# A gated recurrence with residual: x turned on VectorE from small pieces, biases spread by TensorE

## The chip, the core and the metric

The kernel runs on one core of one Trainium2 chip. A core has a matrix engine (TensorE, PE in the profile; its weight loads are PEld), a vector engine (VectorE, DVE), an activation engine (ScalarE, ACT), a general engine (GpSimd, POOL) and SyncE (SP), which here only issues transfers. Each engine runs its own list of instructions in order and waits on semaphores for the others. ACT, POOL and SP each have a queue of transfers, all served by the same 16 DMA engines. Matrix results land in PSUM, everything else lives in SBUF, both with 128 partitions. The metric is the device time of one execution in microseconds. Before the change it is 1333.65 us (median of 3 runs, 1333.27 to 1333.81).

## What is computed

```python
def step(h, inp):                      # x_t, h: 64 x 512; 128 steps
    x_t, prop = inp
    comb = jnp.concatenate([x_t, h], axis=-1)
    z = jax.nn.sigmoid(comb @ Wz + bz)
    r = jax.nn.sigmoid(comb @ Wr + br)
    comb2 = jnp.concatenate([x_t, r * h], axis=-1)
    h_cand = jnp.tanh(comb2 @ Wh + bh)
    h_new = (1.0 - z) * h + z * h_cand
    h_next = jnp.where(prop, jnp.tanh(h_new @ Wp + bp), h_new)
    return (h_next, h_new)             # prop: every fourth step but the last
out = x + transpose(ys)                # x: 64 x 128 x 512, all f32
```

Each weight matrix is 1024 x 512: the upper half meets x, the lower half meets h. Wp is 512 x 512.

## The kernel before

**Layout.** The batch is 64, so a step's 64 x 512 values are kept as 128 partitions x 256 columns: partition s*64+b holds half s of row b. `S = 2` halves, `C = 2` blocks of 128 columns in each, `Q4 = 4` steps to a group. A product needs its left operand turned (columns on the partitions), so every x, h and r*h has to be transposed. `turn` (L212) does it on PE: 8 transposes of bf16 words into the PSUM banks `turn_ps`, and a copy by DVE or ACT. The other half of each `turn_ps` bank, `act_ps`, holds the results of sigmoid and tanh.

**x-part.** The products of x with the upper weights don't depend on the recurrence. They are cut into units and put in `queue`; `fill(n)` issues n of them wherever PE would else wait for the recurrence, `read_out()` issues the copies that empty the four `scratch` banks. Steps 0 to 3 use plain products (`plain`, L428, with readouts L436 and L441 that add the biases). Groups 1 and later use sums and differences of blocks, with fewer products (`batch`, L509; readouts L541 to L552), whose input sums run on POOL (`four`, `sum_raw12`, `sum_raw34`, `sum_s12`) and whose output sums too (`pair_left`, `outer_*`). The weight sums `tw` and `tt` are made during the first steps by DVE (`sum_outer`, L320 to L322; `sum_outer_1`, L326) and POOL (`sum_inner`, L329 to L331).

**Recurrence.** In step t: the R product (four k blocks, `product` at L203), then sigmoid on ACT (L741) and r*h on DVE (L742); three of the four Z products; the turn of r*h and DVE's copies into `rhT` (L210); the last Z product; z, 1-z (L767, L768) and `keep` (L769); units; the H product; tanh (L802) and h on DVE (L803, L808); units; the turn of h, one half copied by DVE, the other by ACT. `seed` (L411) has ACT copy the x-part of the next step into the PSUM slot on which the recurrent products add. The order of all engines is written by hand; each waits only where data or a buffer demands it.

**x, three ways.** The x of steps 0 to 7 (groups 0 and 1, tiles `xr`) is turned on PE by `turn_x` (L243), steps 0 and 1 before the first product, step 2 in step 0 between Z products (L754), steps 3 to 5 in step 0, 6 and 7 in step 1. From group 2 on x takes a path in three pieces: `words_x` (L255) splits each f32 into two 16-bit planes (ACT for groups 2 and 3, POOL later), `planes_x` (L268) turns the planes by one DMA transpose from SP, and `join_x` (L278, L283) has ACT weave the two planes into `xT`. Groups 2 and 3 are loaded early into tiles borrowed from `mb` (`early`), the later ones into one tile `xs`. The inner function `join(n)` (L709) is called at two places of a step, `join(0)` behind r*h and the R seed, `join(1)` behind `keep`, and turns one x at steps with certain numbers `u` in a cycle of eight.

**Loads of the start.** In order on SP: x of steps 0 and 1 (half on ACT's queue), the upper weights of R, Z, H in two pieces of 512 KB each (one on ACT's queue), the lower weights of R and Z, x of steps 2 and 3, the lower weights of H, x of steps 4 to 7, group 2, Wp, the bias of Wp, group 3, group 4. POOL's queue carries, behind a copy into `held` that waits for the first x, h0 (two halves of 64 KB) and the three gate biases, each broadcast from one row to 64 partitions, twice 64 KB each. `idle` (L179) issues matmuls of zeros until the first data arrive. On SP a transfer is issued when the eighth before it on the two hardware queues has landed, which is seen in the issue times (L96 at 14.82 us, when the load of the upper Wh had landed).

Of the kernel before, what the change touches and what calls it, by code (L numbers as in the profile page):

```python
# [9 lines left out]
F32 = mybir.dt.float32  # L10
BF16 = mybir.dt.bfloat16
U16 = mybir.dt.uint16
# [5 lines left out]
def kernel(  # L18
# [41 lines left out]
    R, Z, H_ = range(3)  # L60
# [15 lines left out]
    ones = const.tile([1, B], F32, name="ones")  # L76
# [5 lines left out]
    wx = const.tile([P, K, 3, H], F32, name="wx")  # L82
    wh = [const.tile([P, K, H], F32, name=f"wh_{i}") for i in range(3)]
    wp = const.tile([P, K, H], F32, name="wp")

    tw = {n: const.tile([P, S, S, 3, P], F32, name=f"tw_{n}") for n in (2, 3, 4)}
    tt = const.tile([P, 7, 3, S, 3, P // 2], F32, name="tt")
    gates_in = (Wr, Wz, Wh)
    def load_x(tile_, t0, n, j=0):
        for s in range(S):  # L90
            nc.sync.dma_start(
                out=tile_[s * B : (s + 1) * B, j : j + n, :], in_=x[:, t0 : t0 + n, ts(s, N)]
            )
# [12 lines left out]
    h_init = two.tile([P, N], F32, tag="h", name="h_init")  # L106
    bias_in = const.tile([P, 4, N], F32, name="bias")
# [11 lines left out]
    def load_bias(i, eng):  # L119
        for s in range(S):  # L120
            eng.dma_start(
                out=bias_in[s * B : (s + 1) * B, i, :],
                in_=(br, bz, bh, bp)[i][ts(s, N)]
                .rearrange("(o n) -> o n", o=1)
                .broadcast_to([B, N]),
            )


    held = const.tile([1, 1], F32, name="held")
    nc.gpsimd.tensor_copy(held, xr[0][0:1, 0, 0:1])  # L130
    for s in range(S):
        nc.gpsimd.dma_start(out=h_init[s * B : (s + 1) * B, :], in_=h0[:, ts(s, N)])
    for i in (R, Z, H_):
        load_bias(i, nc.gpsimd)
    for i in range(3):
        for k in (0, 2):
            load_w(wh[i], gates_in[i][D:, :], k, k + 2, nc.sync)
        if i == Z:
            load_x(xr[0], 2, 2, 2)

    dummy = const.tile([1, 1], F32, name="dummy")
    nc.scalar.activation(dummy, ones[:, 0:1], AF.Sigmoid)
    new_xr(1)
    load_x(xr[1], 4, 4)
    early = {}
    for g in (2, 3):
        early[g] = mbp.tile([P, 2, 2, 3, P], F32, tag="mb", name=f"early_{g}").rearrange(
            "p a b c d -> p (a b c d)"
        )[:, : Q4 * N].rearrange("p (t n) -> p t n", t=Q4)
    load_x(early[2], 8, 4)  # L150
    load_w(wp, Wp, 0, 4, nc.sync)
    load_bias(3, nc.sync)
    load_x(early[3], 12, 4)


    rc = ps_c.tile([P, 2, N], F32, name="rc")
# [14 lines left out]

    def cut(ps):
        return ps.rearrange("p (c n) -> p c n", c=C)

    bias0 = bias[:, 0, 0:3, :]
    bias_d = const.tile([P, 3, P], F32, name="bias_d")
# [32 lines left out]
    def copy(eng, dst, src):  # L209
        (eng.copy if eng is nc.scalar else eng.tensor_copy)(dst, src)  # L210
# [21 lines left out]


    xT = {}
    xs = {}
    xw = {}
    xv = {}

    def new_xT(g):
        if g not in xT:  # L240
# [2 lines left out]
    def turn_x(t, eng=nc.scalar):  # L243
        g, i = divmod(t, Q4)
        new_xT(g)
        src = xr[g] if g < 2 else early[g]
        for c in range(C):
            turn(src[:, i, :], xT[g][:, i], c, f"xT_{t}", eng)

    def load_xs(g):  # L250
        if g * Q4 < T:
            xs[g] = one.tile([P, Q4, N], F32, tag="xs", name=f"xs_{g}")
            load_x(xs[g], g * Q4, Q4)

    def words_x(g, i):  # L255

        if g * Q4 >= T:
            return
        if g not in xw:
            xw[g] = one.tile([P, Q4, 2, N], U16, tag="xw", name=f"xw_{g}")  # L260
        src = (early if g < 4 else xs)[g]
        copy(
            nc.scalar if g < 4 else nc.gpsimd,
            xw[g][:, i],
            src[:, i, :].bitcast(U16).rearrange("p (n w) -> p w n", w=2),
        )

    def planes_x(g):  # L268

        if g * Q4 >= T:  # L270
            return
        xv[g] = one.tile([P, Q4, 2, C, P], U16, tag="xv", name=f"xv_{g}")
        nc.sync.dma_start_transpose(
            out=xv[g].rearrange("p t w c n -> p (t w c) n"),
            in_=xw[g].rearrange("p t w n -> p (t w n)"),
        )

    def join_x(g, i):  # L278

        if g * Q4 >= T:  # L280
            return
        new_xT(g)
        nc.scalar.copy(  # L283
            xT[g][:, i].bitcast(U16).rearrange("p c (n w) -> p w c n", w=2), xv[g][:, i]
        )


# [362 lines left out]
    idle(4)  # L650
    turn_x(1, nc.vector)
    idle(8)
    nc.gpsimd.tensor_sub(bias_d, bias[:, 1, 0:3, :], bias0)
    h = h_init
    hT = new_T("hT", "hT_init")
    both = [plain(0), plain(1)]
    for e in range(3):
        for us in both:
            queue.extend(us[4 * e : 4 * e + 4])
        fill(4)  # L660
        if e == H_:
            read_out()
            seed(R, 0)
            seed(Z, 0)
            seed(H_, 0)
        fill(4)
        if e == Z:
            for c in range(C):
                turn(h, hT, c, "hT_init", nc.vector)
# [4 lines left out]
    for t in range(T):  # L674
# [48 lines left out]
        for k in ORDER:  # L723
            product(slots[R], hT, wh[R], k)
        if t < 2:
            if t:
                turn_x(6)
        if t == 1:
            for i in (5, 7):
                sum_inner(i, nc.gpsimd)  # L730
# [20 lines left out]

        for k in ORDER[: 2 if thin else 3]:
            product(slots[Z], hT, wh[Z], k)
        if t == 0:  # L754
            turn_x(2)
        rhT = new_T("rhT", f"rhT_{t}")
        for c in range(C):
            turn(rh, rhT, c, f"rhT_{t}", nc.vector)
# [9 lines left out]
        nc.scalar.activation(slots[Z], slots[Z], AF.Sigmoid, scale=-1.0)  # L768
        nc.vector.tensor_mul(keep, slots[Z], h)  # L769
        join(1)  # L770
        seed(Z, t + 1)
        if prop:
            nc.scalar.copy(cut(slot_p), bias[:, :, 3, :])
# [2 lines left out]
        if t == 0:  # L776
            sum_outer()
            for i in (6,):
                sum_inner(i, nc.gpsimd)
                sum_inner_1(i, nc.gpsimd)  # L780
        if t == 1:
            for n in range(4):
                words_x(2, n)
            planes_x(2)
        elif t == 2:
            for n in range(1, 4):
                join_x(2, n)
            for n in range(2):
                words_x(3, n)
        if not thin:  # L790
            fill(places[0])
        if t == 0:
# [18 lines left out]
        if t == 2:  # L811
            for n in range(2, 4):
                words_x(3, n)
            planes_x(3)
        read_out()
        fill(places[0] if thin else 5 if places[1] > 6 else 4)
        if t == 1:
            turn_x(7)
            sum_raw34(1)
        h = h_new  # L820
        if not last:
            hT = new_T("hT", f"hT_{t}")
            turn(h, hT, 0, f"hT_{t}", nc.vector)
            fill(places[1] if thin else 1 if places[1] > 6 else 2)
            turn(h, hT, 1, f"hT_{t}", nc.scalar)
        if t == 0:
            fill(3)
            turn_x(4)
            fill(3)
        else:  # L830
            fill(places[2] if thin else places[1] - 6)
        if t == 0:
            sum_outer_1()
            for i in (1, 2, 3):
# [11 lines left out]
                turn(h, hT, c, f"hpT_{t}", (nc.vector, nc.scalar)[c])  # L846
            fill(behind[1] if thin else 2)
        if t == 0:
            turn_x(5)
            sum_raw12(1)  # L850
        elif t == 3:
            pair_left(1, 8, 9)
            pair_right(1, 8, 11)
# [38 lines left out]
            sum_s12(even + 2)  # L892
        if t == 2:
            pair_right(0, 1, 10)
        if pair >= 0:
            if u in (1, 2):
                for n in range(2):
                    words_x(even + 2, 2 * (u - 1) + n)
            if u in (5, 6):
                for n in range(2):  # L900
                    words_x(odd + 2, 2 * (u - 5) + n)

        if not last:
            nc.gpsimd.tensor_add(xr[g][:, j, :], xr[g][:, j, :], h_new)  # L904
# [4 lines left out]
        n = 0  # L909
# [14 lines left out]
        if t == 0:  # L924
# [47 lines left out]
```

## Time and profile before

| what | value |
|---|---|
| median of 3 runs | 1333.65 us (1333.27 to 1333.81) |
| profiled execution | 1334.15 us, span 1332.3 us |
| granted clock of TensorE | 0.999 |
| matrix instructions | 15320 |
| DMA: share of 16 engines, all queues | q1 24.7%, q8 0.6%, q10 0.2%, q0 0.1% |
| `join_x` (L283) on ACT | 120 copies, 765 ns each, 91.4 us |
| `words_x` (L210) on POOL | 112 copies, 613 ns each, 65.3 us |
| `words_x` (L210) on ACT | 8 copies, 612 ns each, 4.4 us |
| `turn_x` (L219, from xr) on PE | 64 transposes |
| DMA transpose xv<-xw | 30, 4.3 us from issue to landing (median) |
| biases, POOL's queue | 6 transfers of 64 KB, 6.6 to 6.7 us from issue to landing |

The span is the time from the first to the last instruction of the program; the time of an execution is some 2 us longer. Rows of the profile name a line of the kernel, an engine, an operation and its tiles (written tile first), the number of instructions, their busy time and the mean time of one, and the engine's idle time before them with what ended it. q1 is SP's queue, q10 ACT's, q0 POOL's. The start of a matmul is measured; its end is modelled, since matmuls overlap, so the distance between starts (0.108 us for 256 columns in a run of sixteen that takes 1.73 us) says more of the cost than the duration.

### The profile page before, as it was taken

The page shows a single profiled execution, that of the slowest core. Times are in us where ns is not written, and L with a number is a line of the kernel's source. Part 1 is how long each engine was busy: PE and PEld are TensorE (multiplying, and loading weights), DVE is VectorE, ACT ScalarE, POOL GpSimd, SP SyncE. Part 2 cuts the span into 40 slices and gives each one's busy share as a digit, 9 for nine tenths or more (in the row PEclk, how much of TensorE's full clock was granted, in tenths as well). Part 3 has the DMA queues.
Part 4 walks back from the last instruction along what each step waited for, and adds up shares of the span by engine and source line. Part 5 has one row for each costly group of instructions (what it writes and reads, how often), then busy time and mean ns, then how long its engine had stood idle before and what let it go on. Part 6 is the DMA issues. An engine that isn't in the chain of part 4 may idle for free.

```text
span 1332.3 us, 37617 instructions
## 1 busy us (share of the span) xinstructions
PE 1321.7 (99%) x15320; PEld 1110.8 (83%) x15320; DVE 702.6 (53%) x1870; ACT 635.4 (48%) x1860; POOL 934.9 (70%) x1139
## 2 busy tenths in 40 slices
PE   8999999999999999999999999999999999999998
PEld 5788888888888888888788888888888888888765
DVE  3555555555555555555555555555555555555444
ACT  1554454454544544545444454545545444554433
POOL 4877876777777668776787767786777687767400
PEclk9999999999999999999999999999999999999999
DMA  9322232131221222213122221223212222131300
GB/s 283 55 49 49 49 65 64 33 65 41 57 65 33 66 52 46 65 44 82 37 43 55 64 65 33 59 40 65 65 33 65 49 50 65 33 76 37 98 23 17
DMA packets 119277, 77.79 MB, mean 58 GB/s; under 512 B 65984, under 2 KB 114240, under 8 KB 119104
## 3 DMA queue, kind: packets, MB, share of 16 engines
q1 hardware_dynamic: 118352, 74.14, 24.7%
q8 instruction: 121, 1.98, 0.6%
q10 hardware_dynamic: 496, 0.72, 0.2%
q0 software_dynamic: 256, 0.52, 0.1%
q14 instruction: 52, 0.43, 0.1%
HBM read 42.86 MB, written 16.78 MB: 45 GB/s over the span
## 4 chain that ended last, share of the span: by engine, by line
PE 96%; DMA 2%; DVE 1%; ACT 1%; issue 0%; SPq 0%; DVEq 0%; ACTq 0%
PE rc L194 33%; PE zp L194 20%; PE scratch_q L194 11%; PE scratch_r L194 10%; PE scratch_x L194 10%; PE scratch_a L194 6%; PE turn L219 5%; DMA xr<-in_x_dram 1%; DMA wx<-in_L_cond_Wz_dram 1%; ACT xw L210 0%; ACT xT L283 0%; DVE h L808 0%; DVE turn L803 0%; SPq L96 0%; DVE mb L550 0%
## 5 line engine op out<-in xcount | busy, mean ns | idle before, releaser
L194 PE MATMUL rc<-wh,rhT 128*64 128x256 f32 x2048 | 246.0, 379 | 0.0
L582 POOL TENSOR_TENSOR cp<-mb,mb 128x768 f32<-128x768 f32 x74 | 134.4, 1817 | 102.4 <-ACT rc L411 54.7
L194 PE MATMUL zp<-wh,hT 128*64 128x256 f32 x1536 | 204.3, 379 | 0.0
L194 PEld LDWEIGHTS rc<-wh,rhT 128*64 128x64 f32 x2048 | 168.3, 137 | 40.5
L194 PE MATMUL rc<-wh,hT 128*64 128x256 f32 x1536 | 186.3, 383 | 0.2
L904 POOL TENSOR_TENSOR xr<-xr,h 128x256 f32<-128x256 f32 x127 | 92.5, 728 | 105.3 <-DVE h L808 105.3
L194 PEld LDWEIGHTS rc<-wh,hT 128*64 128x64 f32 x1536 | 121.1, 137 | 36.5 <-issue 9.7
L582 POOL TENSOR_TENSOR cp<-mb 128x768 f32<-128x768 f32 x46 | 83.5, 1815 | 95.1 <-ACT rc L411 93.7
L210 DVE COPY rhT<-turn 128x256 uint16<-128x256 uint16 x256 | 97.6, 420 | 82.2 <-PE turn L219 81.1
L194 PEld LDWEIGHTS zp<-wh,hT 128*64 128x64 f32 x1536 | 118.8, 137 | 25.2
L803 DVE TENSOR_TENSOR turn<-turn,z 128x128 f32<-128x128 f32 x256 | 75.5, 295 | 120.7 <-ACT turn L802 119.0
L741 ACT ACTIVATE turn<-rc 128x128 f32<-128x128 f32 x256 | 55.2, 260 | 171.2 <-issue 111.5
L210 ACT COPY hT<-turn 128x256 uint16<-128x256 uint16 x127 | 47.3, 372 | 165.7 <-DVE hT L210 127.8
L582 POOL TENSOR_TENSOR mb<-mb,mb 128x768 f32<-128x768 f32 x58 | 105.3, 1816 | 9.6 <-DVE mb L552 9.6
L411 ACT COPY rc<-cp 128x256 f32<-128x256 f32 x256 | 96.4, 377 | 26.7 <-DVE cp L436 13.6
L550 DVE TENSOR_TENSOR mb<-scratch_r,cq 128x384 f32<-128x384 f32 (+1 forms) x105 | 58.3, 555 | 92.7 <-ACT cq L549 92.7
L802 ACT ACTIVATE turn<-rc 128x128 f32<-128x128 f32 x256 | 55.5, 260 | 105.3 <-PE rc L194 104.0
L543 DVE TENSOR_TENSOR cx<-scratch_r,cx 128x384 f32<-128x384 f32 (+1 forms) x105 | 58.3, 556 | 88.8 <-ACT cx L541 88.8
L767 ACT ACTIVATE z<-zp 128x256 f32<-128x256 f32 x128 | 49.1, 383 | 94.3 <-PE zp L194 94.2
L283 ACT COPY xT<-xv 128x512 uint16<-128x512 uint16 x120 | 91.4, 765 | 0.0
L808 DVE TENSOR_TENSOR h<-turn,keep 128x128 f32<-128x128 f32 x254 | 74.1, 292 | 15.6 <-DVE turn L803 0.5
L219 PEld LDWEIGHTS <-h 128*64 128x64 bf16 x1016 | 67.6, 110 | 14.0 <-DVE h L808 7.4
(161 smaller groups left out, 3018.0 us busy)
## 6 DMA issues: line engine op xcount, KB each, us to landing
xr<-in_x_dram SPq DMA_DIRECT2D x62, 256.0 KB, 4.1
out_dram<-xr SPq DMA_DIRECT2D x62, 256.0 KB, 3.4
xs<-in_x_dram SPq DMA_DIRECT2D x56, 256.0 KB, 4.2
wx<-in_L_cond_Wz_dram SPq DMA_DIRECT2D x2, 512.0 KB, 8.1
wx<-in_L_cond_Wh_dram SPq DMA_DIRECT2D x2, 512.0 KB, 11.4
wh<-in_L_cond_Wr_dram SPq DMA_DIRECT2D x2, 512.0 KB, 13.2
wh<-in_L_cond_Wz_dram SPq DMA_DIRECT2D x2, 512.0 KB, 15.2
wh<-in_L_cond_Wh_dram SPq DMA_DIRECT2D x2, 512.0 KB, 12.3
```

The lines of the kernel that those rows point to most:

```text
L194: nc.tensor.matmul(ps[s * B : (s + 1) * B], lhsT=lhs, rhs=rhs(s), start=start, stop=True, skip_group_check=True,)
L210: (eng.copy if eng is nc.scalar else eng.tensor_copy)(dst, src)
L219: nc.tensor.transpose(pt[s * B : (s + 1) * B, w, :], words.rearrange("p (n w) -> p w n", w=2)[:, w, :], ident16,)
L283: nc.scalar.copy(xT[g][:, i].bitcast(U16).rearrange("p c (n w) -> p w c n", w=2), xv[g][:, i])
L411: nc.scalar.copy(cut(slots[i]), G[t][:, :, i, :])
L543: nc.vector.tensor_add(T2[n][:, :nm], r_ps[:, :nm], T2[n][:, :nm])
L550: nc.vector.tensor_add(blocks()[:, :nm, 0, 1], r_ps[:, :nm], q2[:, :nm])
L582: nc.gpsimd.tensor_add(dst, a, b)
L802: nc.scalar.activation(pc, slots[H_][:, ts(c, P)], AF.Tanh)
L803: nc.vector.tensor_mul(pc, pc, z[:, ts(c, P)])
L808: nc.vector.tensor_add(h_new[:, ts(c, P)], pc, keep[:, ts(c, P)])
L904: nc.gpsimd.tensor_add(xr[g][:, j, :], xr[g][:, j, :], h_new)
```

## The change

Seven edits:

1. The x of groups 1 and later is loaded by `load_xs` in small pieces: eight transfers for a group, each from 32 rows of the batch into 32 partitions, in runs of 32 f32 (128 bytes), into two alternating tiles of the tags `xs0` and `xs1`. The runs are laid so that each square of 32 x 32 needs only to be turned in itself.
2. `join_x` turns one step's x by one `transpose` on DVE (128 x 256 f32 in squares of 32 x 32) from `xs` into `xT`. `words_x`, `planes_x`, the tiles `early`, `xw` and `xv` and the DMA transposes go.
3. `turn_x` stays for steps 0 to 3 alone. That of step 2 moves from behind three Z products to behind the R product of step 0. Steps 4 and 5 become `join_x` at the end of step 0, 6 and 7 become `join_x` behind `keep` in step 1, with `sum_raw34(1)`.
4. The three gate biases are loaded by POOL as single rows into one partition of `tt`, first on its queue. `spread`, called behind the first eight units, multiplies a column of ones with them into the banks `scratch[3]` and `scratch[1]`, and ACT copies the three results into `bias`. `bias_d` moves behind it.
5. `held`, and with it the load of h0, waits for the first upper weights of R instead of the first x.
6. The x of steps 2 and 3 is loaded ahead of the lower weights of Z instead of behind them.
7. Groups 1 and 2 are loaded into `xs` behind the lower weights of H; then Wp, its bias, and the plain x of steps 4 to 7 for the residual. Groups 3 and 4 are loaded at the ends of steps 1 and 2, the later ones at `u` 3 and 6 as before.

```diff
+    bias_row = tt.rearrange("p a b c d e -> p (a b c d e)")[0:1, : 3 * H].rearrange(
+        "p (i n) -> p i n", i=3
+    )
...
+    for i, b in enumerate((br, bh, bz)):
+        nc.gpsimd.dma_start(out=bias_row[:, i, :], in_=b.rearrange("(o n) -> o n", o=1))
 
     held = const.tile([1, 1], F32, name="held")
-    nc.gpsimd.tensor_copy(held, xr[0][0:1, 0, 0:1])
+    nc.gpsimd.tensor_copy(held, wx[0:1, 1, R, 0:1])
     for s in range(S):
         nc.gpsimd.dma_start(out=h_init[s * B : (s + 1) * B, :], in_=h0[:, ts(s, N)])
-    for i in (R, Z, H_):
-        load_bias(i, nc.gpsimd)
     for i in range(3):
         for k in (0, 2):
             load_w(wh[i], gates_in[i][D:, :], k, k + 2, nc.sync)
-        if i == Z:
+        if i == 0:
             load_x(xr[0], 2, 2, 2)
...
+    def load_xs(g):
+        if g * Q4 < T:
+            xs[g] = one.tile([P, Q4, S * C, 2, 32], F32, tag=f"xs{g % 2}", name=f"xs_{g}")
+            for r in range(4):
+                for bh in range(2):
+                    nc.sync.dma_start(
+                        out=xs[g][ts(r, 32), :, :, bh, :].rearrange("p t k e -> p (t k) e"),
+                        in_=x[ts(bh, 32), g * Q4 : (g + 1) * Q4, :].rearrange(
+                            "b t (k r e) -> r b (t k) e", k=S * C, r=4
+                        )[r],
+                    )
+
+    load_xs(1)
+    load_xs(2)
+    load_w(wp, Wp, 0, 4, nc.sync)
+    load_bias(3, nc.sync)
     new_xr(1)
     load_x(xr[1], 4, 4)
-    early = {}
...
-    load_x(early[2], 8, 4)
-    load_w(wp, Wp, 0, 4, nc.sync)
-    load_bias(3, nc.sync)
-    load_x(early[3], 12, 4)
...
+    def spread(bank, rows, which):
+
+        bank = bank.rearrange("p (i n) -> p i n", i=2)
+        n = len(which)
+        for s in range(S):
+            nc.tensor.matmul(
+                bank[s * B : (s + 1) * B, 0:n, :],
+                lhsT=ones,
+                rhs=bias_row[:, rows, ts(s, N)],
+                start=True,
+                stop=True,
+            )
+        for j, i in enumerate(which):
+            nc.scalar.copy(bias_in[:, i, :], bank[:, j, :])
...
     def join_x(g, i):
 
         if g * Q4 >= T:
             return
         new_xT(g)
-        nc.scalar.copy(
-            xT[g][:, i].bitcast(U16).rearrange("p c (n w) -> p w c n", w=2), xv[g][:, i]
+        nc.vector.transpose(
+            out=xT[g][:, i].rearrange("p c (s b) -> p s c b", s=S),
+            in_=xs[g][:, i].rearrange("p (s c) h e -> p s c (h e)", s=S),
         )
...
+        if e == R:
+
+            spread(scratch[3], slice(0, 2), (R, H_))
+            spread(scratch[1], slice(2, 3), (Z,))
+            nc.gpsimd.tensor_sub(bias_d, bias[:, 1, 0:3, :], bias0)
...
         for k in ORDER:
             product(slots[R], hT, wh[R], k)
         if t < 2:
-            if t:
-                turn_x(6)
+            if t == 0:
+                turn_x(2)
...
         nc.vector.tensor_mul(keep, slots[Z], h)
         join(1)
+        if t == 1:
+            join_x(1, 2)
+            join_x(1, 3)
+            sum_raw34(1)
...
-        if t == 1:
-            for n in range(4):
-                words_x(2, n)
-            planes_x(2)
-        elif t == 2:
+        if t == 2:
             for n in range(1, 4):
                 join_x(2, n)
-            for n in range(2):
-                words_x(3, n)
...
-        if t == 1:
-            turn_x(7)
-            sum_raw34(1)
...
-        if t == 0:
-            fill(3)
-            turn_x(4)
-            fill(3)
-        else:
-            fill(places[2] if thin else places[1] - 6)
+        fill(places[2] if thin else places[1] - 6)
...
         if t == 0:
-            turn_x(5)
+            join_x(1, 0)
+            join_x(1, 1)
             sum_raw12(1)
...
-        if t == 0:
-            load_xs(4)
+        if t in (1, 2):
+            load_xs(t + 2)
         if pair >= 0:
             if u == 3:
-                planes_x(even + 2)
                 load_xs(odd + 2)
             elif u == 6:
-                planes_x(odd + 2)
                 load_xs(even + 4)
```

The steps of the schedule that call `join` (its table of steps and `u`) are unchanged.

More of the change, by code (lines that the diff above doesn't have):

```diff
@@ L142 @@
     nc.scalar.activation(dummy, ones[:, 0:1], AF.Sigmoid)
+    xs = {}
+    def load_xs(g):
[13 more added lines that the diff above has]
+    load_bias(3, nc.sync)
     new_xr(1)
     load_x(xr[1], 4, 4)
-    early = {}
[L146 to L149, printed above, removed]
-    load_x(early[2], 8, 4)
-    load_w(wp, Wp, 0, 4, nc.sync)
-    load_bias(3, nc.sync)
-    load_x(early[3], 12, 4)
     rc = ps_c.tile([P, 2, N], F32, name="rc")
@@ L234 @@
     xT = {}
-    xs = {}
-    xw = {}
-    xv = {}
     def new_xT(g):
@@ L245, in turn_x @@
         new_xT(g)
-        src = xr[g] if g < 2 else early[g]
+        src = xr[g]
         for c in range(C):
             turn(src[:, i, :], xT[g][:, i], c, f"xT_{t}", eng)
[L250 to L276, printed above, removed]
     def join_x(g, i):
@@ L652 @@
     idle(8)
-    nc.gpsimd.tensor_sub(bias_d, bias[:, 1, 0:3, :], bias0)
     h = h_init
@@ L753 @@
             product(slots[Z], hT, wh[Z], k)
-        if t == 0:
-            turn_x(2)
         rhT = new_T("rhT", f"rhT_{t}")
@@ L810 @@
             seed(H_, t + 1)
[L811 to L814, printed above, removed]
         read_out()
         fill(places[0] if thin else 5 if places[1] > 6 else 4)
-        if t == 1:
-            turn_x(7)
-            sum_raw34(1)
         h = h_new
@@ L894 @@
             pair_right(0, 1, 10)
[L895 to L901, printed above, removed]
         if not last:
@@ L923 @@
             load_x(xr[g + 1], (g + 1) * Q4, Q4)
-        if t == 0:
-            load_xs(4)
+        if t in (1, 2):
+            load_xs(t + 2)
         if pair >= 0:
             if u == 3:
-                planes_x(even + 2)
                 load_xs(odd + 2)
             elif u == 6:
-                planes_x(odd + 2)
                 load_xs(even + 4)
```

## Prediction

> **What bounds the kernel now.** I read the busy shares first, then a table of stretches, then the chain of waits at the start, then the timeline of single engines.
>
> ```profile
> PE 1321.7 (99%) x15320; PEld 1110.8 (83%) x15320; DVE 702.6 (53%) x1870; ACT 635.4 (48%) x1860; POOL 934.9 (70%) x1139
> ...
> 8.00:12.50 4.50, 3.98 (x38) 2.37 (x37) 0.00 (x0) 0.00 (x0) 0.56 (x2) 1.00 1.07 298
> 12.50:25.00 12.50, 10.65 (x98) 6.06 (x99) 3.29 (x8) 1.87 (x6) 9.20 (x10) 1.00 1.06 338
> 25.00:44.00 19.00, 18.65 (x218) 14.72 (x220) 15.22 (x27) 6.35 (x21) 9.61 (x12) 1.00 0.81 176
> ...
> 100.00:420.00 320.00, 320.00 (x3756) 276.29 (x3753) 172.77 (x461) 157.15 (x460) 237.48 (x290) 1.00 0.25 54
> ```
>
> The stretch rows give length, then busy time and count of PE, PEld, DVE, ACT and POOL, granted clock, DMA share, GB/s. From 100 us on PE fills the stretch, and the waits view has no wait of PE between 100 and 1240 us. Whatever the change takes from ACT or POOL there is worth nothing; only PE instructions that go, or new waits of PE, count. Before 25 us the DMA share is full and PE has holes: the start is bound by loads.
>
> ```profile
> 2.94 9.46 DMA wx<-in_L_cond_Wz_dram
> ...
> 12.42 12.43 DMA xr<-in_x_dram
> ...
> 25.32 0.38 ACT xT L210
> ...
> 45.27 2.18 ACT xw L210 x4
> ```
>
> The chain (start, length, what) runs through Wz, the x of steps 2 and 3, the ACT copy that turns x of step 2, and ACT's `words_x`.
>
> **The loads of the start.** The biases are now 384 KB of broadcast on POOL's queue; the change reads three rows of 2 KB. What that frees is seen in three stretches:
>
> ```profile
> 9.00:14.00 5.00, 4.48 (x42) 2.74 (x40) 0.00 (x0) 0.00 (x0) 0.00 (x0) 1.00 1.06 272
> 15.00:20.00 5.00, 4.88 (x52) 2.85 (x48) 2.80 (x6) 1.06 (x3) 4.30 (x5) 1.00 1.05 386
> 25.00:29.00 4.00, 3.65 (x44) 2.83 (x46) 2.23 (x5) 1.68 (x5) 0.68 (x1) 1.00 1.13 221
> ...
> q1 hardware_dynamic: 473, 0.91, 70.7%
> q0 software_dynamic: 229, 0.45, 35.0%
> ```
>
> The two queue rows are those of 9 to 14 us: SP's queue moved 0.91 MB there while POOL's moved 0.45. In 15 to 20 us SP's alone moved 1.92 MB. So 0.45 MB of POOL's traffic cost SP's stream 1.01 MB, at 386 GB/s 2.6 us; all 0.52 MB cost about 3.0, and the biases' three quarters 2.2 us. By bytes alone 0.39 MB would be 1.0 us; I take 2.2, the measured loss, and keep 1.0 as the low end.
>
> Now the last load that step 0 waits for. Before: Wz's second recurrent half lands at 23.69, x of steps 2 and 3 at 24.85 (landings read from the trace). The change swaps them; the sum ahead of the last of them is the same, so the last now lands at 24.85 - 2.2 = 22.65. PE before:
>
> ```profile
> 23.73 1.08 PE L194 MATMUL zp<-wh,hT_init 128*64 128x256 f32 x8 [1.13 <-DMA wh<-in_L_cond_Wz_dram]
> ...
> 24.98 0.42 PE L219 MATMUL turn<-ident,xr 128*64 128x128 bf16 x8 [0.17 <-DMA xr<-in_x_dram]
> ...
> 25.75 0.58 PE L219 MATMUL turn<-ident,rh 128*64 128x128 bf16 x8 [0.35 <-ACT xT L210]
> ...
> 26.57 0.38 PE L194 MATMUL scratch_q<-wx,xT 128*64 128x256 f32 x1
> ```
>
> After: PE starts at 7.82 as before (Wr; POOL's bulk traffic began only at 8.3). The eight units of the R gate take 2 x 1.73 (16 matmuls take 1.73 in the chain), to 11.28. `spread` adds two pairs of matmuls, one of 512 columns, one of 256: a pair of 256 takes 1.73/4 = 0.43, so 0.86 + 0.43 = 1.3, to 12.6. Z units 3.46, hT_init 0.22, H units 3.46, R product of step 0 1.73, to 21.45; `turn_x(2)`, whose x is there by then, 0.22; first Z product 0.43, to 22.1. There it waits for Wz until 22.7 (landing plus 0.05). Two Z products 0.86, turn of rh 0.25, last Z product 0.43: filling starts at 24.24 instead of 26.57. **Gain 2.3.** The 1.3 us of `spread` lie ahead of the wait and are hidden, 0.55 to spare. Without any wait PE could not be there before 23.75 (rh's own path through ACT, now behind `turn_x(2)`'s two copies): ceiling 2.8. With 1.0 for the biases: 1.1.
>
> Moved past POOL's queue: `h_init` waits for Wr (7.8) instead of x (4.2). It landed 5.8 after issue, so 13.7 and 14.4; PE wants it at 16.04. Cost 0, 1.6 us to spare. `bias_d` and the three ACT copies (0.38 each) end by 14; their first reader is at 17.
>
> **PE instructions that go.** `turn_x` of steps 4 to 7 goes: 8 transposes each, 0.22 us in the chain. **Gain 4 x 0.22 = 0.88**, certain. The ACT copies behind the one of step 7 also held PE: the last matmul ahead of it starts at 49.07, turn of h at 50.23, 1.16 us for 0.16 + 0.30 of work. The wait is shared with h, which came late because ACT ran `words_x` up to 47.45, and with it the readouts `cx`, `cq`, tanh, and then DVE. With those copies gone, `cx` is read when its units end, h is ready before PE asks. **Gain 0.70** (low end 0). The same at step 2: PE waits for h at 67.66 and 68.19, excess 0.41, behind `words_x` at 63.98 to 65.1. **Gain 0.41** (low end 0). The wait at 75.65 for DVE's L550 stays: it hangs on the rhT copies.
>
> **What DVE gets.** 124 turns of 128x256 f32. The trace has no such operation; nearest are DVE operations of 128x256 at 0.42 (L769, L441). Bounds: 0.33 (only the 256 columns and a little) and 0.84 (two passes). I take 0.42: 52 us in all, DVE from 53% to 57%. Where do they stand? `join(0)` is between rh and the copies of rhT, `join(1)` behind keep:
>
> ```profile
> 453.54 0.49 DVE L742 TENSOR_TENSOR rh<-turn,hprop 128x128 f32<-128x128 f32 x2 [0.40 <-ACT turn L741]
> 454.65 0.76 DVE L210 COPY rhT<-turn 128x256 uint16<-128x256 uint16 x2 [0.62 <-PE turn L219]
> 455.89 0.42 DVE L769 TENSOR_TENSOR keep<-zp,hprop 128x256 f32<-128x256 f32 x1 [0.48 <-ACT zp L768]
> ```
>
> The hole ahead of rhT is 0.62, and the H product that reads rhT starts at 455.29, 0.22 behind the first copy's end (455.07). So a turn of up to 0.84 costs nothing there; behind keep DVE is idle 1.29 until 457.60. Steady state: 0.
>
> At the end of step 0 it is tighter. `join_x(1, 0)` and `(1, 1)` stand behind the weight sums:
>
> ```profile
> 39.56 1.02 DVE L334 TENSOR_TENSOR wx<-wx 128x384 f32<-128x384 f32 x2
> ...
> 41.10 0.41 DVE L441 TENSOR_TENSOR cp<-scratch_x,bias 128x256 f32<-128x256 f32 x1
> 42.48 0.49 DVE L742 TENSOR_TENSOR rh<-turn,h 128x128 f32<-128x128 f32 x2 [0.97 <-ACT turn L741]
> ```
>
> DVE is busy without a break from 36.55 to 41.51, so all shifts by 2.3. Sums end at 38.27, joins at 39.1, readouts L436 and L441 at 40.1, rh at 40.35 and 40.6. PE, 2.3 + 0.44 earlier, ends the R product at 38.74 and three Z products at 40.04, and turns rh's second half only at 40.65. **Loss 0.45** (0 with short turns, 1.3 with turns of 0.84). POOL's s12r, s34r and `pair_left` follow 1.2 to 3.5 us earlier, ahead of their readers.
>
> **The small pieces.** One group of four steps is 4,096 packets of 128 B on 16 engines, 256 each. Nearest row: the DMA transpose of 48 to 52 us, 256 B each:
>
> ```profile
> q1 hardware_dynamic: 2080, 0.52, 94.3%
> ```
>
> 94.3% of 16 x 4 us over 2,080 packets is 29 ns each; 256 x 29 = 7.4 us a group. The load of Wh ends at 29.14 - 2.2, about 26.6 to 27; with 1.5 us to land, group 1 is there at 35.5, wanted at 38.3 by DVE; group 2 at 43, wanted at 50.6 (first join of step 2). Hidden, and 7.4 us in 41 later. The Trainium skill speaks against it: "DMA: Bandwidth & Descriptors", Specifications, wants at least 512 B for line rate and has smaller ones do a read-modify-write. Taken as twice the row, an estimate, 58 ns: group 1 at 43, group 2 at 58, and DVE, with PE behind it, waits 7 us in all. By the row 0, by the rule a loss of 7. I take the row, which has small packets with all that they cost; no run yet shows 128 B from HBM. The low end is bytes alone, 1.4 us a group; the high end 82 ns, what a packet cost at 25 to 29 us, where x was read in 1 KB rows (1.13 x 64 us over 886 packets).
>
> **Sum.** 2.3 + 0.88 + 0.70 + 0.41 - 0.45 = 3.84. The profiled execution took 1334.15 (span 1332.3), half a us over the median of 1333.65; so 1330.3 by the one, **1329.8** by the median. Own range: best 2.8 + 0.88 + 1.11 = 4.8, worst 1.1 + 0.88 - 1.3 = 0.7; likely 1328.9 to 1331.2.
>
> **Rivals.**
> - *Small pieces late (slower).* The DVE queue stands behind group 1, then group 2, at step 2. It decides from (50.6 + 3.8 - 28.1)/0.512 = 51 ns a packet; at 58 ns 7 late less 3.8 is about 1337, at 82 near 1349. For: x in long strides is slow already (221 against 386 GB/s). Against: 256 B packets at 29 ns. 15%.
> - *DVE turns over 0.84.* At 1.2 us each of 60 `join(0)` holds rhT 0.36: 22 us, 1352. Against: nothing of 256 columns on DVE takes over 0.42. 5%.
> - *The start does not follow* (h_init late, or Wz gains by bytes alone), and the two h waits stay: 0.7 to 2.6 us, about 1331.8. 20%.
>
> The forecast has 60%. A difference of 0.2% is 2.7 us, about what can be told from none. Faster 0.60; same 0.19, the third rival; slower 0.21, the first two and a little of the unforeseen. The range 1328.6 to 1336 holds forecast, third rival and the mild part of the first.
>
> **What would show it.** Right: filling of step 0 starts near 24.2; no `xw`, `xv` rows; no wait of PE at 49 and 67; a wait of about 0.4 for rh near 40; DVE turns near 0.42; x group 1 landed by 38, group 2 by 50. Wrong: DVE idle behind a DMA of xs, packets of 128 B over 51 ns, or PE waits that recur past 100 us.

## The result and the profile after

| | before | after |
|---|---|---|
| median of 14 runs each | 1333.72 us (1332.73 to 1336.55) | 1330.46 us (1329.96 to 1331.19) |
| ratio | | 0.9974, 95% interval 0.9967 to 0.998 |
| profiled execution | 1334.15 us, span 1332.3 | 1330.92 us, span 1328.9 |

The changed kernel is 3.26 us faster by the medians and 3.4 by the spans of the two profiled executions; 3.84 was forecast. Its profiled execution has the longest span of its 14 (1327.6 to 1328.9, median 1328.2). The busy shares, from the page of the changed kernel:

```profile
PE 1320.0 (99%) x15296; PEld 1114.5 (84%) x15296; DVE 748.0 (56%) x1994; ACT 552.5 (42%) x1727; POOL 871.0 (66%) x1024
```

ACT lost 83 us of work, POOL 64, DVE gained 45, and PE, which sets the time, lost 1.7. The table of stretches of the changed kernel, columns as before:

```profile
8.00:12.50 4.50, 3.27 (x30) 2.02 (x32) 0.00 (x0) 0.00 (x0) 0.00 (x0) 1.00 1.06 356
12.50:25.00 12.50, 12.50 (x128) 7.87 (x130) 3.66 (x10) 3.34 (x11) 9.90 (x10) 1.00 1.07 300
25.00:44.00 19.00, 18.90 (x200) 12.96 (x198) 16.51 (x32) 4.71 (x15) 9.54 (x11) 1.00 0.61 133
...
100.00:420.00 320.00, 320.00 (x3754) 276.31 (x3752) 184.22 (x492) 137.53 (x429) 219.72 (x261) 1.00 0.19 40
```

The steady stretch is as full as before. From 12.5 to 25 us PE, which had been idle for 1.85 us, is now never idle; the loads no longer hold it. The hole has moved to 8 to 12.5 us, where PE lost 0.52 before and loses 1.23 now. The waits of PE between 0 and 100 us in the changed kernel (total, times, longest; left out is one of 1.2 for DVE's zeros, which all these kernels have):

```profile
PE scratch_q L224 <- DMA wx<-in_L_cond_Wr_dram: 1.7, 1, 1.7
...
PE scratch_r L224 <- DVE mb L550: 0.2, 1, 0.2
```

The waits for Wz, for x, for ACT's copy and for h are gone, L550's stayed, and one for Wr has grown from 0.4 to 1.7. Where the time came from is read by following the same matmul of each step in both traces; the difference of its start times changes only where something was gained or lost. Each row gives what was gained (-) or lost (+) between its place and the one above:

| place | forecast | measured |
|---|---|---|
| start, to the filling of step 0 (26.57 to 25.04) | -2.33 | -1.53 |
| `turn_x` 4, 5 gone, to step 1's R product (39.55 to 37.58) | -0.44 | -0.45 |
| `turn_x` 6 gone, to its Z products (41.51 to 39.30) | -0.22 | -0.22 |
| new wait for rh, to its H product (46.20 to 44.24) | +0.45 | +0.24 |
| `turn_x` 7 and the wait for h gone, to step 2's R product (51.12 to 48.17) | -0.92 | -0.99 |
| wait for h of step 2 gone, to step 3's R product (68.98 to 65.53) | -0.41 | -0.50 |
| from there to the end | 0 | 0: the difference stays between -3.35 and -3.54, at the end -3.39 |

Only the start is off by more than 0.21 in this execution; run 5 shows that the start differs from one execution to the next. The timeline of PE there, changed kernel (start, length, what, idle before it):

```profile
6.89 0.63 PE L224 MATMUL scratch_q<-wx,xT 128*64 128x256 f32 x4
9.23 1.51 PE L224 MATMUL scratch_q<-wx,xT 128*64 128x256 f32 x12 [1.70 <-DMA wx<-in_L_cond_Wr_dram]
10.57 1.90 PE L224 MATMUL scratch_a<-wx,xT 128*64 128x256 f32 x16
12.40 1.07 PE L195 MATMUL scratch_x<-tt,ones 1*64 1x512 f32 x4
13.31 0.60 PE L195 MATMUL scratch_r<-tt,ones 1*64 1x256 f32 x4
```

PE starts its units at 6.89, stops after four matmuls until the second half of the upper Wr (ACT's queue) lands at 9.18, and then runs without a break to 40.77. `spread`, from 12.40 to 13.84, lies in that unbroken run, so its 1.44 us are on the path.

### The profile page after: what moved, and what is told of

It is laid out like the page before. It is cut to its first block, busy times and chain, and to the rows that moved or that the text cites. A ratio compares the mean times of both kernels' runs of the same rounds, so it can differ in the third digit from the quotient of the medians.

```text
span 1328.9 us, 37667 instructions
## 1 busy us (share of the span) xinstructions
PE 1320.0 (99%) x15296; PEld 1114.5 (84%) x15296; DVE 748.0 (56%) x1994; ACT 552.5 (42%) x1727; POOL 871.0 (66%) x1024
## 4 chain that ended last, share of the span: by engine, by line
PE 96%; DMA 2%; SPq 1%; DVE 0%; issue 0%; ACTq 0%; ACT 0%; DVEq 0%
PE rc L224 33%; PE zp L224 20%; PE scratch_q L224 11%; PE scratch_r L224 11%; PE scratch_x L224 11%; PE scratch_a L224 6%; PE turn L249 5%; SPq L156 1%; DMA xr<-in_x_dram 1%; DMA wx<-in_L_cond_Wr_dram 1%; DMA bias<-in_L_cond_bp_dram 0%; DVE wx L334 0%; DVE turn L803 0%; ACTq L114 0%; DVE xT L282 0%
## 5 line engine op out<-in xcount | busy, mean ns | idle before, releaser
L550 DVE TENSOR_TENSOR mb<-scratch_r,cq 128x384 f32<-128x384 f32 (+1 forms) x105 | 58.3, 555 | 90.5 <-ACT cq L549 89.0
L249 PE MATMUL turn<-ident,h 128*64 128x128 bf16 x1016 | 77.8, 220 | 0.3 <-DVE h L808 0.2
```

The lines of the kernel that those rows point to most:

```text
L249: nc.tensor.transpose(pt[s * B : (s + 1) * B, w, :], words.rearrange("p (n w) -> p w n", w=2)[:, w, :], ident16,)
L550: nc.vector.tensor_add(blocks()[:, :nm, 0, 1], r_ps[:, :nm], q2[:, :nm])
```

## The experiments

Each changes the changed kernel, or the kernel before where it says so, and computes the whole output. The first theory was the one that the timeline gives: PE's start is now held by one late half of Wr, everything behind it is PE's own work. Its rivals were that the loads still set the start, and that the gains outside the start were something else than the steps of the forecast. Runs 1 to 4, 5 to 8 and 9 to 12 shared a chip each; the medians of the kernel before on them were 1333.81, 1333.53 and 1334.02.

**1. Both halves of Wr on SP's queue.**

```diff
-                wx[:, :, i, :], gates_in[i], k, k + 2, nc.scalar if (i, k) == (R, 2) else nc.sync
+                wx[:, :, i, :], gates_in[i], k, k + 2, nc.sync
```

> The changed kernel with both halves of the upper Wr on SP's queue (the second was on ACT's). Theory: the changed kernel's start is held by that half alone, which landed at 9.18 us because it shared the engines with Wz; on one queue it lands behind the first half near 7.0 to 7.5, PE loses its 1.85 us wait, and filling of step 0 starts near 23.0 to 23.4 instead of 25.04, where the lower Wz (21.3) and rh are next: about 1.7 to 2.0 us under the changed kernel, 1328.6. Rival (the bytes ahead of PE's first units are what counts, in whatever queue): no change, 1330.5. Rival (the late landing was chance of one execution): the changed kernel's usual time already has it early, and this is the same within 0.3.

Measured: 1330.88 us (1329.57 to 1331.18), ratio 0.9974 [0.9964, 0.9985]. The expectation was missed. The second half landed at 8.60, later than expected; PE waited 1.1 us instead of 1.7 and filling of step 0 began at 24.45 instead of 25.04, but the time cannot be told from the changed kernel's. One queue isn't the cure. The third rival, that the late landing was the chance of one execution, is left standing; run 5 takes it up.

**2. The biases broadcast again, all else as changed.**

```diff
-    for i, b in enumerate((br, bh, bz)):
-        nc.gpsimd.dma_start(out=bias_row[:, i, :], in_=b.rearrange("(o n) -> o n", o=1))
...
-    nc.gpsimd.tensor_copy(held, wx[0:1, 1, R, 0:1])
+    nc.gpsimd.tensor_copy(held, xr[0][0:1, 0, 0:1])
...
+    for i in (R, Z, H_):
+        load_bias(i, nc.gpsimd)
...
-            spread(scratch[3], slice(0, 2), (R, H_))
-            spread(scratch[1], slice(2, 3), (Z,))
```

> The changed kernel with the biases broadcast on POOL's queue behind h0, and held waiting for x, as before the change; no spread. Theory: loads of the start land 2.2 to 3.5 us later, the lower Wz near 24.0 to 24.8, filling starts near 25.7 to 26.4 instead of 25.04: 0.7 to 1.4 us slower than the changed kernel, 1331.2 to 1331.9. Rival (the start's gain comes from the order of x of steps 2 and 3 and from its turn, not from the biases): no change, 1330.5. Rival (spread's 1.4 us of PE lie on the path once PE is the limit): 1.4 us faster, 1329.1.

Measured: 1331.40 us (1330.96 to 1332.06), ratio 0.998 [0.9972, 0.9989], as expected. The waits of PE up to 100 us, first of those for loads:

```profile
PE zp L223 <- DMA wh<-in_L_cond_Wz_dram: 1.3, 2, 0.7
...
PE scratch_q L223 <- DMA wx<-in_L_cond_Wr_dram: 1.1, 1, 1.1
PE rc L223 <- DMA wh<-in_L_cond_Wr_dram: 0.8, 1, 0.8
PE scratch_q L223 <- DMA wx<-in_L_cond_Wz_dram: 0.4, 1, 0.4
```

With 384 KB of broadcasts back on POOL's queue the loads hold PE again at three products where the changed kernel has no wait: lower Wz, lower Wr and upper Wz. The lower Wz lands at 24.56 instead of 21.32, 3.2 us later, but only 1.13 us of this reach PE (filling at 26.17 against 25.04): in the changed kernel Wr's late half and PE's own work, `spread` in it, have taken the loads' place. Both numbers compare single executions. In the seven profiles with this start (the changed kernel and runs 5, 7 and 9 to 12) the lower Wz lands at 21.32 to 23.12, median 21.80, and filling starts at 23.58 to 25.04, median 24.08; against these medians the rows are worth 2.8 us of loading, of which 2.1 reach PE in this profile and 1.3 the end, by the medians of the spans (1329.5 against 1328.2).

**3. The kernel before with the start alone** (bias rows and `spread`, `held`, the order of x and Wz, `turn_x(2)`); x stays on its old ways.

```diff
+        if e == R:
+            spread(scratch[3], slice(0, 2), (R, H_))
+            spread(scratch[1], slice(2, 3), (Z,))
...
+        if t == 0:
+            turn_x(2)
+        if t == 1:
+            turn_x(6)
...
-        if t == 0:
-            turn_x(2)
         rhT = new_T("rhT", f"rhT_{t}")
```

> The kernel before with the edits of the start alone: biases as rows and spread, h0 behind Wr, x of steps 2 and 3 ahead of the lower Wz and turned behind the R product. x goes its old ways (PE turns, planes, joins on ACT). Theory: filling of step 0 starts near 25.0 as in the changed kernel, the other 1.9 us of the change are missing: 1.5 under the kernel before, 1332.2. Rival (all of the change's gain is in the start): 1330.4. Rival (none of it is): 1333.7.

Measured: 1331.90 us (1331.47 to 1332.73), ratio 0.9984 [0.9975, 0.9993], as the theory has it, though filling started at 24.20 and not near 25.0. The shift is 2.36 at step 0 and between 2.17 and 2.46 through all later steps: next to nothing of the start is given back. Two waits of PE tell where the rest is:

```profile
PE scratch_q L214 <- DMA wx<-in_L_cond_Wr_dram: 0.6, 1, 0.6
PE turn L239 <- DVE h L831: 0.4, 2, 0.2
```

The waits for h near 47 and 65 us are still there, so it is the part of the change that concerns x that removes them (no run takes ACT's `words_x` out alone). Its wait for Wr was 0.6 where the changed kernel's was 1.7; that is why this half alone has a start 0.8 us better than the whole.

**4. The kernel before with both halves of Wr on SP's queue**, by the edit of run 1.

> The kernel before with both halves of the upper Wr on SP's queue. Theory: there the lower Wz (23.69) and x of steps 2 and 3 (24.85) are the limit, and the same bytes lie ahead of them, so the edit that gains near 2 us in the changed kernel gains nothing here: within 0.4 of 1333.7. Rival (Wr's place in the queues is what starts PE in either kernel): 1.0 to 2.0 faster, or slower where it lands later.

Measured: 1334.39 us (1334.03 to 1335.79), ratio 1.0004 [0.9995, 1.0013]: no gain, as expected, though a little above the 0.4 us allowed. There the lower Wz (landed 23.43) still set the start.

**5. The changed kernel once more, with nothing edited.** Between the profiles so far the second half of Wr had landed anywhere from 7.4 to 9.2 us. If that differs from execution to execution, the size of the start is partly chance.

> The changed kernel once more, to see whether its second half of Wr lands late (9.18 us in its profile, 7.41 before the change) in every execution. Theory: SP and ACT issue their halves within 0.05 us of each other, and which goes first differs from execution to execution; with ACT first the half lands near 7.7, PE runs unbroken from 7.9 and the time is 1.0 to 1.3 lower, so the times spread over more than 1 us. Rival: POOL's three row loads at 1.5 us make ACT the later one in each execution; then 9.2 again and the same time.

Measured: 1329.98 us (1329.56 to 1331.43), ratio 0.9974 [0.9964, 0.9984]. The same code, the first line of PE's units in its timeline:

```profile
7.34 1.95 PE L224 MATMUL scratch_q<-wx,xT 128*64 128x256 f32 x16
```

No wait at all: the two halves landed at 6.88 and 7.30, PE runs unbroken from 7.34, and step 0 stands 2.98 us ahead of the kernel before instead of 1.53 (span 1327.4). What differs is how far ACT's issue is ahead. Where it stands at 1.51 to 1.53 and SP's at 1.55 to 1.56, the second half lands at 5.9 to 8.0 and the first at 7.3 to 8.2 (nine profiles, the kernel before among them); where ACT's stands at 1.55 to 1.57, within 0.01 us of SP's, the second half lands at 9.1 to 9.3 (three profiles, the changed kernel's first among them). The order could be seen, not set; what decides it stays open.

**6. Units of step 0 by halves of Wr**, those that need only the first half ahead of those that need the second.

```diff
-        for us in both:
-            queue.extend(us[4 * e : 4 * e + 4])
+        if e == R:
+            queue.extend(us[n + m] for n in (0, 1) for us in both for m in (0, 2))
+        else:
+            for us in both:
+                queue.extend(us[4 * e : 4 * e + 4])
```

> The changed kernel with the first eight units in another order: the four of both steps that need the first half of Wr, then the four that need the second. Theory (behind the change PE's work from the first units on is the limit of the start): PE has 1.73 us of work before it needs the second half, so 1.3 us of the wait in front of it go when it lands near 9.2, and all of a shorter wait: filling of step 0 near 23.7, 1329.2, up to 1.3 under the changed kernel. Rival (the lower weights land last, as before the change): the wait moves to the lower Wr or Wz, no change.

Measured: 1329.99 us (1329.63 to 1330.84), ratio 0.9973 [0.9962, 0.9984]. The second half landed at 9.33, as late as in any profile, and PE no longer waits for it; step 0 stands 2.67 us ahead. So in these profiles the wait for Wr is what cost the start. The medians of this and of run 5 agree to 0.01 us: a change that pays only in some executions is too small for the times here.

**7. One weight sum moved from ahead of the joins at the end of step 0 to behind rh of step 1**; a single execution.

```diff
+        if t == 1:
+            sum_inner_1(3, nc.vector)
         seed(R, t + 1)
...
-            for i in (1, 2, 3):
+            for i in (1, 2):
                 sum_inner_1(i, nc.vector)
```

> The changed kernel with one of DVE's three weight sums (0.5 us) moved from before the turns of x of steps 4 and 5 to behind r*h of step 1. Theory: the 0.25 us that PE waits for rh near 40.4 is DVE's queue, the two turns in it; it goes, and the shift of step 1's H product grows from 0.24 less than that of its Z product to the same: 0.25 to 0.3 in all, 1330.2. Rival (rh waits for ACT's sigmoid): no change at that place.

Measured: 1329.34 us, span 1327.6. From step 1's Z to its H product the changed kernel's lead shrinks by 0.24; here it grows by 0.13. The wait for rh is gone, worth 0.37 at its place.

**8. Runs 6 and 7 together, and in step 3 `read_out()` ahead of the turn of rh** (the wait on L550).

```diff
+        if t == 3:
+            read_out()
         rhT = new_T("rhT", f"rhT_{t}")
```

> The changed kernel with the order of units by halves of Wr, the late weight sum, and in step 3 the readout of the units ahead of the copies of rhT instead of behind them (it held PE 0.37 us near 72). Theory: the three are at different places and add: 1.3 or less + 0.25 + 0.37, 1328.5 to 1329.2. Rival: a wait that goes at the start comes back at the next load; then 0.6 at most, 1329.9.

Measured: 1329.14 us (1328.13 to 1329.41), ratio 0.9963 [0.9951, 0.9976]: the best version, 4.4 us under the kernel before and 0.84 under the changed one on the same chip. Its stretches:

```profile
25.00:44.00 19.00, 19.00 (x204) 13.36 (x202) 16.54 (x32) 4.91 (x15) 11.24 (x13) 1.00 0.63 139
44.00:70.00 26.00, 26.00 (x318) 23.71 (x314) 12.71 (x35) 8.21 (x26) 23.83 (x29) 1.00 0.24 39
70.00:100.00 30.00, 30.00 (x355) 26.12 (x352) 17.63 (x48) 12.79 (x40) 24.20 (x26) 1.00 0.27 54
```

PE fills each of them; one wait of 0.3 us for Wr is the only one left between 7 and 100 us. There less time can now come only from fewer matmuls, or from an earlier start. (The end is another matter: in the last 28.9 us of the changed kernel PE is busy for 23.66, and none of these edits touches it.)

**9. and 10. The DVE turn issued twice, and three times.**

```diff
+        for _ in range(2):
             nc.vector.transpose(
```

> The changed kernel with each turn on DVE issued twice (0.87 us in place of 0.43). Theory: the hole ahead of the copies of rhT is 0.62 us and the H product has 0.22 more, so 0.87 costs at most 0.03 at 60 places; the two turns at the end of step 0 add 0.87 ahead of rh: 0.9 to 2.7 slower than the changed kernel, 1331.2 to 1333.0. Rival (DVE has no room; each turn is on the path): 124 x 0.43 = 53 us slower.

> The changed kernel with each turn issued three times (1.30 us). Theory: the cover of 0.84 us ends; each of some 60 turns between r*h and rhT holds the H product by 0.46, those behind keep are still hidden (1.29): 27 us, and 1.7 at the end of step 0: near 1359. Rival (the cover is shared with later work, and units fill the wait): under 5 us, 1335.

Measured: 1341.09 us (1340.56 to 1342.01), ratio 1.0051 [1.0036, 1.0066], and 1369.11 us (1368.51, 1369.72), ratio 1.0261 [1.024, 1.0281]. Twice was expected to be hidden in the steady state, and isn't: each `join(0)` costs 0.10 to 0.20 us, on average 0.155, besides 0.96 in step 1. Three times costs 0.64 at each on average, more than the 0.46 expected. DVE's timeline with the turn doubled, and the H product behind it:

```profile
453.57 0.92 DVE L283 STREAM_TRANSPOSE xT<-xs 128x256 f32<-128x256 f32 x2
454.42 0.72 DVE L240 COPY rhT<-turn 128x256 uint16<-128x256 uint16 x2
...
454.95 1.30 PE L224 MATMUL rc<-wh,rhT 128*64 128x256 f32 x10
```

The pair takes 0.92 and loses 0.155, so what a turn may take unseen is on average 0.92 - 0.155 = 0.77, not the forecast's 0.84. That was read off as 0.62 of idle time plus 0.22 from the first copy's end to the H product. Here the first copy, at the 0.42 of a single one, ends at 454.84, and H, which is late in this run, starts at 454.95: of the 0.22, 0.11 was the way from DVE to PE and no slack. Run 10 has 0.12 at the same place (copy 464.52 + 0.42, H at 465.06).

**11. and 12. Smaller pieces: 16 transfers of 64-byte runs for a group, and 32 of 32-byte runs**, instead of 8 of 128 bytes.

```diff
+                    for q in range(4):
                         nc.sync.dma_start(
-                            out=xs[g][ts(r, 32), :, :, bh, :]...
+                            out=xs[g][ts(r, 32), :, :, bh, ts(q, 8)]...
```

> The changed kernel with pieces of 64 bytes: twice the transfers and packets for x. Theory: 16 issues of 0.53 us and 8,192 packets near 11 ns (5.6 us on 16 engines) for a group; group 1 lands near 31.5 and group 2 near 40, wanted near 38.9 and 50: no change, within 0.4 of the changed kernel. Rival (small pieces already weigh on the start or on the other loads): 2 us or more slower.

> The changed kernel with pieces of 32 bytes: four times the transfers and packets. Theory: now SP's issues, 32 of 0.53 us for a group, outlast the cover: group 1 lands near 40.5 (wanted 38.9), group 2 near 57.5 (wanted 50.5 and what was lost at the first): DVE, and PE behind it, waits 5 to 7 us in all: 1335.5 to 1337.5, all of it before 70 us, nothing later. Rival (packets cost by bytes, issue is cheap): no change. Rival (the load of packets weighs on every group): tens of us.

Measured: 1330.62 us (1329.82 to 1331.12), ratio 0.9973 [0.9962, 0.9984], no change, though the groups landed some 3 us later than expected (34.42 and 43.84); and 1344.44 us (1343.86 to 1346.04), ratio 1.0078 [1.0063, 1.0093], twice the loss expected. The first join with 32-byte runs, DVE, and then the stretches around it:

```profile
43.36 0.77 DVE L285 STREAM_TRANSPOSE xT<-xs 128x256 f32<-128x256 f32 x2 [5.34 <-DMA xs<-in_x_dram]
```

```profile
39.00:45.00 6.00, 0.76 (x8) 0.23 (x4) 1.64 (x5) 0.38 (x1) 0.71 (x2) 0.88 0.52 29
45.00:50.00 5.00, 4.71 (x34) 3.49 (x36) 2.30 (x8) 1.03 (x3) 4.84 (x8) 0.50 0.56 33
...
87.30:92.00 4.70, 4.33 (x36) 2.86 (x38) 3.19 (x9) 0.75 (x2) 3.16 (x7) 0.64 0.54 31
```

The waits of PE from 30 to 100 us:

```profile
PE turn L252 <- DVE rh L749: 5.5, 1, 5.5
PE scratch_r L227 <- POOL cp L585: 3.1, 1, 3.1
```

PE stands still for 5.5 us behind DVE, and for 3.1 us more before 87.3, behind sums on POOL that late x had pushed back (POOL's `s12r` waits 8.4 us for a turned x). The clock column shows what the expectation left out: behind each standstill TensorE was granted half speed. At 0.50 over 5 us PE does 2.5 us less work; at 0.64 over 4.7 us, 0.36 x 4.7 = 1.7 less. 5.5 + 3.1 + 2.5 + 1.7 = 12.8, less 1.0 for a start that had ACT's half of Wr early, makes 11.8; the span is 12.3 longer than the changed kernel's. The share of the engines stayed at a half (0.52 to 0.56), so it isn't bandwidth: SP needs 0.53 us to issue one transfer, 32 of them 17 us for a group, and group 2 landed 17.5 us behind group 1 (60.70 against 43.24).

## Why the prediction was right, and where it was off

**Start (-2.33 forecast, -1.53 in the profiled execution).** The forecast had "the last now lands at 24.85 - 2.2 = 22.65", a wait for Wz until 22.7 behind which "the 1.3 us of `spread`" are hidden, and "PE starts at 7.82 as before". In the changed kernel's profile its sum differs in three places:
- PE's start was not a constant. The eight units of the R gate take 3.60 us and, with the wait for Wr in them, ended at 12.40, as if PE had started at 8.80: 0.98 lost.
- PE's chain of work was longer than its sum: `spread` 1.44 instead of 1.3, the R units 3.60 instead of 3.46, and some 0.14 in smaller pieces: 0.42 lost.
- The wait for Wz, 0.60 in the forecast, never came: the lower Wz landed at 21.32, and PE wanted it later. So no load behind Wr was the limit any more, and the cover of `spread` was gone.

0.98 + 0.42 - 0.60 = 0.80, the whole difference.

This execution was an unlucky one. Seven profiles have the same work on PE up to the filling of step 0 and the same loads up to the lower weights (the changed kernel and runs 5, 7, 9, 10, 11 and 12). Their starts gain 1.53, 2.98, 2.48, 2.51, 2.17, 1.83 and 2.54 us, median 2.48, one of them more than the forecast's ceiling of 2.8. In runs 5, 7, 9, 10 and 12 filling starts 16.24 to 16.25 us behind PE's first unit, wherever between 7.34 and 8.15 that lies: PE's own chain, with `spread` in it, is the limit, and the landing of Wr sets it going. (In run 11, 0.2 us of waiting for Wz comes on top.) That the median is so near the forecast is in part luck: its mechanism, a last wait for Wz that hides `spread`, was wrong, and the wait that did not come and the longer chain nearly cancel. The size of the loads' gain was about right: the lower Wz landed 1.7 to 3.5 us before the 24.85 of the old order, with 2.2 forecast.

The median time, 0.66 us above the forecast, can't be laid on the start. By the spans the forecast was met: the changed kernel's median is 1328.2, that of the kernel before 1332.0, 1331.7 and 1332.2 on the three chips of the experiments, a gain of 3.5 to 4.0. What is missing lies mostly outside the span. The kernel before takes 1.73 to 1.92 us more than its span (55 runs), the changed kernel 1.76 to 2.89, median 2.27. Runs 2 and 3, each without one part of the change, have medians of 1.82 and 1.79. The forecast had nothing there; what takes the additional 0.4 us stays open.

**`turn_x` of steps 4 to 7 (0.88).** Measured 0.45 + 0.22 + some 0.22 in the next row. Run 3, which lacks it, keeps a constant shift instead.

**The waits for h (0.70 and 0.41).** 0.99 - 0.22 = 0.77 and 0.50. Run 3 shows them still there with x on its old ways, and the changed kernel's list of waits doesn't have them. That it was ACT's `words_x`, as the forecast says, is read from the chain of the kernel before and was not tested alone.

**The new wait for rh (+0.45).** There, at half the size, 0.24. The order was as forecast, DVE without a break from the weight sums to rh (changed kernel):

```profile
38.95 0.76 DVE L282 STREAM_TRANSPOSE xT<-xs 128x256 f32<-128x256 f32 x2
39.64 0.65 DVE L436 TENSOR_TENSOR cp<-scratch_a,bias 128x512 f32<-128x512 f32 x1
40.21 0.40 DVE L441 TENSOR_TENSOR cp<-scratch_x,bias 128x256 f32<-128x256 f32 x1
40.55 0.47 DVE L746 TENSOR_TENSOR rh<-turn,h 128x128 f32<-128x128 f32 x2
```

DVE's queue was 0.2 us later than forecast at rh, PE 0.8, by the late start; the wait is what lay between them. Run 7, a single execution, shows that it was DVE's queue: with one weight sum less ahead of the joins the place gives 0.37 back.

**DVE's turns (0.42 taken, 0.434 measured, 0.398 to 0.446).** The nearest row, another operation of 128x256 f32, was right to 3%. In the steady state they are free, as forecast: no wait of PE from 100 to 1240 us. The rival of longer turns is refused by the measured 0.434; runs 9 and 10 show that its mechanism is real and where it begins (0.77).

**Small pieces (29 ns a packet taken).** The changed kernel's transfers from 44 to 50 us (packets, MB, share of 16 engines):

```profile
q1 hardware_dynamic: 4224, 0.52, 56.2%
```

0.562 x 16 x 6 us over 4,224 packets is 12.8 ns. The row taken was more than twice too high, and 58 ns, the estimate made from the Trainium skill ("DMA: Bandwidth & Descriptors", Specifications: transfers under 512 B do a read-modify-write), over four times; run 11 gives 10.8 ns at 64 bytes and run 12 gives 8.9 at 32, so in these reads nothing doubles a packet's price. Group 1 landed at 28.49 and group 2 at 34.72, forecast as 35.5 and 43; hidden, with more to spare. (The forecast's 1.5 us to land stood there without a row; the quickest piece took 2.0 from the start of its issue to its landing.) The rival of late pieces fell, but run 12 shows what it would have looked like, by SP's issues and not by packets.

**Chances.** The likeliest case came true. None of the three rivals came. In the profiled execution the start fell 0.8 us short, but not for a reason that the third rival names: h0 was not late, Wz gained more than by its bytes, and both waits for h went. That PE's start hangs on the issue of two queues was in no rival.

## What to carry to other kernels

Where loads are made faster, look at once for what is late next: here it was the busy engine's own chain, 16.24 us from its first unit on, in which the small work that replaced the loads (1.44 us of matmuls) had no cover any more. One profile is one execution: the start's gain lay between 1.5 and 3.0 us in seven of them. Cover is read from when the waiting instruction could start, not from the end of the one before it: of a gap of 0.22 us, 0.11 was the way from one engine to the next. And the price of a wait on TensorE includes the clock behind it: 8.6 us of standstill cost some 4.2 more at half speed.

## What the hardware showed that was not expected

- **Two queues, 0.05 us apart.** Two transfers of 512 KB issued on two queues within 0.05 us don't share evenly: the half on ACT's queue landed at 5.9 to 8.0 when its issue was 0.02 to 0.05 us ahead of SP's, and at 9.1 to 9.3 when the two were within 0.01 us. On one queue the second half came at 8.60 (run 1) and 8.03 (run 4). Why that isn't as early as with ACT's ahead is open.
- **Clock.** After 5.5 us without a matmul the granted clock was 0.50 over the next 5 us, and after 3.1 us it was 0.64 over 4.7 us. The Trainium skill ("TensorE: Matmul & The Clock Gate", Part 1: The HAM clock gate) has half speed after a window of about 3.4 us without work; it agrees with the first, and the second shows that 3.1 us can be enough.
- **Broadcast loads** of 64 KB each from one row of 2 KB cost the other queue more than their bytes: with 384 KB of them the lower Wz landed at 24.56 (run 2), without them at 21.32 to 23.12, median 21.80 (the seven profiles): 1.4 to 3.2 us, where at 386 GB/s they would take 1.0.
